# Sums over scores by halves of 512 columns, with gc tiles of two batches and gathers four slots ahead

## The chip, the cores and the metric

The kernel runs on one core of a Trainium2 chip, from one program in one launch. Its time is the device time of an execution in microseconds (us); lower is better. TensorE is called PE, VectorE DVE, ScalarE ACT, GpSimd POOL and SyncE SP, as in the profile. Everything is float32.

## What is computed

Sixteen graphs (batches) of 1024 nodes with 256 features each go through four layers; all share one 1024x1024 matrix adj, which has about 17 entries that aren't zero in a row. The reference, cut to what matters:

```python
# layer 0: a score for every edge, then two sums over neighbours
pre_u, pre_v = h @ W1[:d], h @ W1[d:]
S   = sigmoid(relu(pre_u[:, :, None] + pre_v[:, None] + b1) @ W2 + b2)
a_t = einsum('buv,bud->bvd', S * adj, h)
m_t = einsum('uv,bud->bvd', adj, h) * h
z   = beta1 * h + beta2 * (a_t @ Wa + ba) + beta3 * (m_t @ Wm + bm)
# layer 1
z = z + relu((adj @ z) @ W.T + b)
# layers 2 and 3: attention, each with its own weights
feats  = z @ W1.T;  f1 = feats @ W2 + b2
coefs  = softmax(leaky_relu(f1[:, :, None] + f1[:, None, :]) + adj)
z = coefs @ feats + bias2 + z
```

## The kernel before

The batches are worked in four groups of four (GB). A first part, `score_free`, makes for all 16 batches what layer 0 has besides the scores, and keeps it in DRAM (zb_d, and h·Wa as hw_d). Then each group runs `with_edges`, which adds the sums over scores onto z, and `group_layers`, which makes layers 1 to 3. The last group is worked in pairs of batches (`far_ahead`, `pair_layers`).

**Scores, on the side.** `score_steps` makes a group's scores one group ahead. A step takes one neighbour of each of 128 nodes in four batches: POOL gathers rows of v_d into a slot tile z of 4112 bytes a partition (`fetch`, L945), DVE takes a maximum, a minimum and a product with the tile u (L1065 to L1067), ACT sums the features of the four batches (L1033). Every 16 or 4 steps there are a tanh and a product with adj, and POOL scatters the scores into a dense matrix in DRAM, dense_d, whose innermost index is the batch (L950). 608 steps are made in all. The pool of slots has 6 tiles; LEAD = 5 says that the gather of step n + 5 is issued in step n, so it needs the slot that step n - 1 has left. The class `Side` emits so many of these steps beside each part of the main work as the table PACE says, and `paced` makes an instruction wait for a matmul some places back in PE's order, so that the side work keeps pace.

**Sums over scores, before.** For each group there are four quarters of 256 columns (v) and eight tiles of 128 rows (ut). One load (SP, `load_gd`, L1147, pool gd of four tiles) brings 128 x 256 x 4 scores; one copy turns them from column by batch into batch by column (gc, pool of two tiles): DVE makes it for ut 2, 4, 6 and 7 (L1496), ACT for the others (L1498). Then eight products, four batches by two halves of the output features, add into eight banks, each half full; that is all the banks there are. A float32 product shows as two matmul instructions in the profile. After the eighth ut DVE adds the eight banks onto z (L1521). Loads of the next z and of the turned adj into `ea`, and ACT's exponential of it, are strewn between.

**Other users of what changes.** `adj_stream` feeds layer 1 (seven products of quarters in place of eight, `seven`) with blocks of adj and of sums of its quarters: it puts pairs of blocks into gc tiles and single ones into a pool of three. Where it has more room (the first three groups) every second name goes to a wide tile. In the last group `by_lists` makes the neighbour sums of layer 1 for six tiles of nodes by gathering rows of y_d into the same slots (L945), adding them on DVE (L1716, L1718, L1714) and storing partial sums in part_d (L1722, on SP's queue).

Of the kernel before, what the change touches and what calls it, by code (L numbers as in the profile page):

```python
# [11 lines left out]
F32 = mybir.dt.float32  # L12
# [5 lines left out]
P = 128  # L18

GB = 4  # L20
# [12 lines left out]
HOLD = 52  # L33
FAR = 6
AHEAD = 3
LEAD = 5
LAG = 1
SOUGHT = 6
PLAIN = 3
# [41 lines left out]
def gnn_stack_kernel(  # L81
# [27 lines left out]
    nc = tc.nc  # L109
# [814 lines left out]
    with tc.If(listed > 0) as arm:  # L924
        with ExitStack() as stack:
# [4 lines left out]


            zs = stack.enter_context(tc.tile_pool(name="zs", bufs=2, reuse_waits="tile"))
            slot_pool = stack.enter_context(tc.tile_pool(name="slots", bufs=6, reuse_waits="tile"))
            wide_z = stack.enter_context(tc.tile_pool(name="wide_z", bufs=4, reuse_waits="tile"))
            wide_t = stack.enter_context(tc.tile_pool(name="wide_t", bufs=5, reuse_waits="tile"))
            psum_pool(stack, "banks", 8)
            gd_pool = stack.enter_context(tc.tile_pool(name="gd", bufs=4, reuse_waits="tile"))
            gc_pool = stack.enter_context(tc.tile_pool(name="gc", bufs=2, reuse_waits="tile"))
            searched = set()
            put = [Scatters(tc, f"scores {g}") for g in range(NGR)]  # L940
            finished = []
# [228 lines left out]
            with ExitStack() as first:  # L1170
# [60 lines left out]
                def score_free():  # L1231
# [58 lines left out]
                    for b in range(B):  # L1290
                        h, hT = kept.pop(0)
                        if b == 1:
                            nat = load_naturals(stage)
                            w1 = own1.tile([P, DH, 2 * R + D], F32, name="w1p")
                            nc.sync.dma_start(w1.rearrange("p c k -> p (c k)"), w_d)
                        mT = new_mT(pools)
                        rest = along_seven(b)
                        if b == B - 1:
                            first_hw.extend(load_hw(i) for i in range(GB - 1))
                        if b < PLAIN - 1:  # L1300
                            yield from first_turned(messages(pools, h, hT, mT=mT))
                        elif b == PLAIN - 1:
                            yield from last_plain(h, hT, mT)
                            sums = sums_of_adj()
                            rest = iter(())
                        else:
                            adding = itertools.chain(
                                adding, feature_sums(quarter, kept[0][0]) if b + 1 < B else iter(())
                            )
                            yield from mixed_in(messages(pools, h, hT, sums, quarter, mT), rest)  # L1310
                        if b == B - 1:
                            first_gd.extend(load_gd(0, 0, ut) for ut in range(4))
                        yield from rest
# [166 lines left out]
                yield 1.2  # L1480

            def exponential(jt):
                paced(nc.scalar.activation(ea[:, jt, :], ea[:, jt, :], AF.Exp), 16)

            def with_edges(g, hw, z):

                doing[0] = "edges"
                for v in range(N // QN):
                    cols = slice(v * QN, (v + 1) * QN)
                    acc = [[bank() for _ in range(DH)] for _ in range(GB)]  # L1490
                    for ut in range(NT):
                        gd = first_gd.pop(0) if first_gd else load_gd(g, v, ut, back=BACK)
                        gc = gc_pool.tile([P, GB, QN], F32, tag="gc", name="gc")
                        by_batch = gd.rearrange("p n i -> p i n")
                        if ut in (2, 4, 6, 7):
                            paced(nc.vector.tensor_copy(gc, by_batch), 16)  # L1496
                        else:
                            paced(nc.scalar.activation(gc, by_batch, AF.Copy), 16)  # L1498
                        for i in range(GB):
                            for eh in range(DH):  # L1500
                                product(
                                    acc[i][eh][:, :QN], hw[i][:, ut, eh * P : (eh + 1) * P], gc[:, i, :],
                                    start=ut == 0, stop=ut == NT - 1,
                                )
                        if z_loads and ut % 2 == 0:
                            load, *what = z_loads.pop(0)
                            paced(load(*what), 12)
                        if (to_load or to_exp) and ut % 2 and v:
                            if v > 1 and to_exp:
                                exponential(to_exp.pop(0))  # L1510
                            if to_load:
                                jt = to_load.pop(0)
                                paced(nc.sync.dma_start(ea[:, jt, :], adjT_d[jt]), 16)
                                to_exp.append(jt)
                        yield 3.4 if g or v else 1
                    if v == N // QN - 1:
                        while to_exp:
                            exponential(to_exp.pop(0))
                    for i in range(GB):
                        for eh in range(DH):  # L1520
                            nc.vector.scalar_tensor_tensor(  # L1521
                                z[i][:, eh, cols], acc[i][eh][:, :QN], zbias[:, eh : eh + 1], z[i][:, eh, cols],
                                ALU.add, ALU.add,
                            )

            def projected(z, keep=None, ticks=False, y=None):

# [45 lines left out]
            def adj_stream(room):  # L1573
# [31 lines left out]
                def block(name, k):  # L1605

                    if used:
                        q, was = used.pop()
                        if roomy is not None:
                            ask_for(q + 2, was) if q % 2 or was == 1 else was > 1 and single()  # L1610
                        elif was == 1:
                            ask_for(q + 2, was)
                        elif was > 1:
                            single()
                    used.append((names.index(name), k))
                    return ready[name, k]
# [13 lines left out]
                single(True)  # L1630
                single(True)
                ask(names[1], 0, HT if roomy is not None else 1, True)
                if roomy is not None:
                    ask(names[2], 0, first=True)
                single(True)
                return block

            def neighbours_by_seven(y, z, t, block):
# [42 lines left out]
            def by_lists(msg):  # L1681
# [16 lines left out]
                def fetch_row(t, k):  # L1698
# [4 lines left out]
                    else:  # L1703
                        gather(z, y_d, lists(t)[1][:, k : k + 1])

                for step in todo[:LEAD]:
                    fetch_row(*step)
                for n, (t, k) in enumerate(todo):
# [10 lines left out]
                            to, z, lists(t)[3][:, k : k + 1], to, ALU.mult, ALU.add  # L1719
                        ))  # L1720
                    if t >= NT and k == QUAD - 1:
                        nc.sync.dma_start(part_d[(t - NT) * P : (t - NT + 1) * P, :], to)  # L1722
                    yield 1.0

            def from_lists(z, msg):
# [145 lines left out]
            def soon(g):  # L1871

                if g in finished:
                    first_gd.extend(load_gd(g, 0, ut) for ut in range(4))

            def far_ahead(z, main):

# [161 lines left out]
```

## Time and profile before

| | us |
|---|---|
| median of three runs | 3041.68 |
| lowest and highest run | 3033.42, 3042.52 |
| the profiled execution | 3062.02 |
| its span, first to last instruction | 3059.9 |

The mean granted clock of TensorE in the profiled execution is 0.997. An engine's busy time is the union of its instructions; a group's line reads: line, engine, operation, written tile and read tiles, shapes, count, busy time in us and mean length of one in ns, then the idle time of the engine just before these instructions and what ended most of it. A matmul's mean length is longer than its share of the busy time, since matmuls overlap. In the view by windows a row has the stretch, its length, the busy time of PE, PEld, DVE, ACT and POOL with the number of instructions, the granted clock, the busy share of the DMA engines and GB/s. In a timeline a row has start, length, engine, line, operation, tiles and shape, and in brackets the idle time before and what ended it.

### The profile page before, as it was taken

How to read it: one execution, taken by the hardware profiler on the slowest of the kernel's cores; microseconds unless marked ns; L12 is line 12 of the kernel's file. 1: busy time of each engine (PE TensorE's matmuls, PEld its weight loads, DVE VectorE, ACT ScalarE, POOL GpSimd, SP SyncE). 2: the span in 40 equal slices, each digit the busy share in tenths (PEclk: the TensorE clock that was granted, in tenths of full speed). 3: DMA queues.
4: the chain of work that ended last, by engine and by line, in shares of the span. 5: the costliest groups of instructions: out<-in, count | busy, mean ns of one | idle time of the engine just before them, and what ended most of it. 6: DMA issues, size and time to landing. Idle time of an engine off the chain costs nothing. (4 is left out here: it accounts for less than half of the span.)

```text
span 3059.9 us, 41657 instructions
## 1 busy us (share of the span) xinstructions
PE 2994.9 (98%) x11774; PEld 2147.0 (70%) x11774; DVE 2080.4 (68%) x4093; ACT 1816.5 (59%) x6461; POOL 1717.0 (56%) x1481
## 2 busy tenths in 40 slices
PE   8999999999999999999999999999999999989999
PEld 5545555555557657888775788887578888848888
DVE  8877666666665678887667788766677752268844
ACT  3337665666666767887766678776667733214342
POOL 1137577677665667667676667666666520167500
PEclk9999999999999999999999999999999999999999
DMA  8899999889899976578998666898865445485500
GB/s 295 316 355 328 311 310 300 276 256 277 251 347 328 307 263 183 172 218 290 302 296 273 179 182 195 290 299 280 276 202 168 141 158 161 154 271 162 161 1 29
DMA packets 321145, 731.52 MB, mean 239 GB/s; under 512 B 50749, under 2 KB 145018, under 8 KB 315786
## 3 DMA queue, kind: packets, MB, share of 16 engines
q0 software_dynamic: 128064, 388.90, 42.1%
q1 hardware_dynamic: 154634, 271.98, 26.5%
q10 hardware_dynamic: 38208, 67.91, 5.9%
q8 instruction: 95, 1.56, 0.2%
q14 instruction: 144, 1.18, 0.1%
HBM read 592.10 MB, written 136.53 MB: 238 GB/s over the span
## 5 line engine op out<-in xcount | busy, mean ns | idle before, releaser
L1033 ACT ACTIVATE z<-z 128x257 f32<-128x257 f32 x2432 | 983.8, 410 | 529.7 <-DVE z L1067 290.8
L141 PE MATMUL bank<-feats,m 128*128 128x257 f32 x4096 | 912.3, 381 | 8.2 <-DVE m L1464 5.7
L141 PEld LDWEIGHTS bank<-feats,m 128*128 128x128 f32 x4096 | 769.5, 190 | 121.8 <-DVE m L1464 9.1
L945 POOL DMA_INDIRECT z<-v_d,slot_v x512 | 602.0, 1176 | 406.1 <-issue 149.0
L950 POOL DMA_INDIRECT dense_d<-gt,slot_at x512 | 595.2, 1162 | 220.3 <-issue 98.9
L1065 DVE TENSOR_TENSOR z<-z,u 128x580 f32<-128x580 f32 x608 | 461.2, 759 | 354.3 <-PE bank L141 259.2
L141 PE MATMUL bank<-gc,hw 128*128 128x256 f32 x2048 | 455.1, 384 | 20.8 <-ACT gc L1498 18.3
L1033 ACT ACTIVATION_READ_ACCUMULATOR z<-z 128x1 f32 x2432 | 467.1, 192 | 0.0
L141 PEld LDWEIGHTS bank<-gc,hw 128*128 128x128 f32 x2048 | 390.3, 192 | 85.0 <-ACT gc L1498 25.2
L1464 DVE SCALAR_TENSOR_TENSOR m<-rho,tau,adj_sb 128x512 f32<-128x512 f32 x512 | 375.0, 745 | 108.4 <-PE bank L141 98.5
L1066 DVE TENSOR_TENSOR z<-z,u 128x448 f32<-128x448 f32 x608 | 376.3, 619 | 0.0
L141 PE MATMUL bank<-w1p,hT 128*128 128x385 f32 x1024 | 340.1, 486 | 1.1 <-ACT hT L153 1.1
L141 PEld LDWEIGHTS bank<-w1p,hT 128*128 128x128 f32 x1024 | 193.1, 189 | 148.0 <-issue 22.0
L141 PE MATMUL bank<-g_wT,z 128*128 128x257 f32 x1024 | 231.0, 380 | 3.7 <-DVE z L1650 2.2
L141 PE MATMUL bank<-adj_sb,h 128*128 128x512 f32 x504 | 223.3, 592 | 1.1 <-DMA h<-in_x_dram 1.1
L141 PEld LDWEIGHTS bank<-g_wT,z 128*128 128x128 f32 x1024 | 191.9, 190 | 34.9 <-issue 4.4
L1498 ACT ACTIVATE gc<-gd 128x1024 f32<-128x1024 f32 x64 | 132.4, 2069 | 105.0 <-PE bank L141 90.3
L372 ACT ACTIVATE st<-bank 128x385 f32<-128x385 f32 x256 | 122.5, 483 | 105.7 <-PE bank L141 72.4
L141 PEld LDWEIGHTS bank<-adj_sb,h 128*128 128x128 f32 x504 | 95.5, 190 | 115.9 <-issue 106.5
L945 POOL DMA_INDIRECT z<-v_d,x_node x96 | 116.5, 1214 | 99.4 <-PE bank L141 32.4
L1067 DVE TENSOR_TENSOR z<-z,sign 128x128 f32<-128x128 f32 x608 | 172.2, 283 | 0.0
L1496 DVE COPY gc<-gd 128x1024 f32<-128x1024 f32 x64 | 71.5, 1118 | 139.4 <-PE bank L141 109.6
(248 smaller groups left out, 3311.4 us busy)
## 6 DMA issues: line engine op xcount, KB each, us to landing
gd<-dense_d SPq DMA_DIRECT2D x128, 512.0 KB
dense_d<-zero ACTq DMA_DIRECT2D x64, 512.0 KB
h<-in_x_dram SPq DMA_DIRECT2D x19, 1024.0 KB
u_d<-st SPq DMA_DIRECT2D x128, 128.5 KB
v_d<-st SPq DMA_DIRECT2D x128, 128.5 KB
u<-u_d POOLq DMA_DIRECT2D x32, 514.0 KB
hw_d<-st SPq DMA_DIRECT2D x128, 128.0 KB
zb_d<-zb ACTq DMA_DIRECT2D x16, 1024.0 KB
```

Source lines behind the costliest of these rows:

```text
L141: recent.append(nc.tensor.matmul(*args, **kw))
L372: nc.scalar.activation(st[:, cols], ps[:, :half], AF.Copy)
L945: return paced(nc.gpsimd.indirect_dma_start(out=dst, out_offset=None, in_=src[:], in_offset=bass.IndirectOffsetOnAxis(ap=at, axis=0), **how,))
L950: return paced(nc.gpsimd.indirect_dma_start(out=dst[:], out_offset=bass.IndirectOffsetOnAxis(ap=at, axis=0), in_=src, in_offset=None,))
L1033: nc.scalar.activation(zk[:, c, :], zk[:, c, :], AF.Copy, accum_out=s[:, k, c : c + 1])
L1065: paced(nc.vector.tensor_tensor(big, big, uk[:, :, :BIG], ALU.max))
L1066: paced(nc.vector.tensor_tensor(low, low, uk[:, :, BIG:], ALU.min))
L1067: nc.vector.tensor_tensor(mixed, mixed, sign[:, None, :].to_broadcast([P, GB, MIXED]), ALU.mult)
L1464: nc.vector.scalar_tensor_tensor(m, r[:, cols], ta[:, kt : kt + 1], ea[:, kt, cols], ALU.max, ALU.mult)
L1496: paced(nc.vector.tensor_copy(gc, by_batch), 16)
L1498: paced(nc.scalar.activation(gc, by_batch, AF.Copy), 16)
```

## The change

Five things are changed, the rest of the program is as it was.

- `with_edges` goes by halves of 512 columns. For each ut two loads bring the two quarters; a gc tile holds 512 columns of two batches, so that each load is copied in two parts, and each gc tile is filled by two copies. Of the four copies of a ut ACT makes one and DVE three. A product is 512 columns wide and fills a bank. The first two batches' banks are added onto z after their last product, the other two's after the copies of the next half's first ut.
- The gc pool has three tiles, the slot pool five in place of six, and LEAD is 4.
- Where an instruction was held to a matmul 24, 16 or 12 places back in this part, it is held to one 12, 8 or 6 back, since a product is twice as wide.
- `adj_stream` asks for three gc blocks at its start and runs three names ahead with them.
- `by_lists` stores part_d from ACT's queue, three steps after the sum is made.

```diff
-LEAD = 5
+LEAD = 4
...
-slot_pool = ... name="slots", bufs=6
+slot_pool = ... name="slots", bufs=5
-gc_pool = ... name="gc", bufs=2
+gc_pool = ... name="gc", bufs=3
...
-first_gd.extend(load_gd(0, 0, ut) for ut in range(4))
+first_gd.extend(load_gd(0, q, ut) for ut in range(2) for q in range(2))
...
 def with_edges(g, hw, z):
-    for v in range(N // QN):
-        acc = [[bank() for _ in range(DH)] for _ in range(GB)]
-        for ut in range(NT):
-            gd = first_gd.pop(0) if first_gd else load_gd(g, v, ut, back=BACK)
-            gc = gc_pool.tile([P, GB, QN], F32, tag="gc", name="gc")
-            by_batch = gd.rearrange("p n i -> p i n")
-            if ut in (2, 4, 6, 7):
-                paced(nc.vector.tensor_copy(gc, by_batch), 16)
-            else:
-                paced(nc.scalar.activation(gc, by_batch, AF.Copy), 16)
...
+    PB = GB // 2
+    acc, ended = {}, []
+
+    def copied(gds, pair):
+        gc = gc_pool.tile([P, GB, QN], F32, tag="gc", name="gc")
+        gc = gc.rearrange("p a b -> p (a b)").rearrange("p (i n) -> p i n", n=HN)
+        for q, gd in enumerate(gds):
+            to = gc[:, :, q * QN : (q + 1) * QN]
+            by_batch = gd.rearrange("p n i -> p i n")[:, pair * PB : (pair + 1) * PB, :]
+            if pair or q:
+                paced(nc.vector.tensor_copy(to, by_batch), 8)
+            else:
+                paced(nc.scalar.activation(to, by_batch, AF.Copy), 8)
+        return gc
+
+    def onto_z(pair, v):
+        cols = slice(v * HN, (v + 1) * HN)
+        for i in range(pair * PB, (pair + 1) * PB):
+            for eh in range(DH):
+                nc.vector.scalar_tensor_tensor(
+                    z[i][:, eh, cols], acc[i, eh], zbias[:, eh : eh + 1], z[i][:, eh, cols],
+                    ALU.add, ALU.add,
+                )
+
+    for v in range(NV):
+        for ut in range(NT):
+            gds = [first_gd.pop(0) if first_gd else load_gd(g, 2 * v + q, ut, back=12) for q in range(2)]
+            for pair in range(2):
+                gc = copied(gds, pair)
+                if ut == 0:
+                    while pair and ended:
+                        ended.pop()()
+                    for i in range(pair * PB, (pair + 1) * PB):
+                        for eh in range(DH):
+                            acc[i, eh] = bank()
+                for i in range(pair * PB, (pair + 1) * PB):
+                    for eh in range(DH):
+                        product(
+                            acc[i, eh], hw[i][:, ut, eh * P : (eh + 1) * P], gc[:, i - pair * PB, :],
+                            start=ut == 0, stop=ut == NT - 1,
+                        )
...
+                if ut == NT - 1 and not pair:
+                    onto_z(0, v)
+                yield 3.4 if g or v or ut >= NT // 2 else 1
+        ended.append(functools.partial(onto_z, 1, v))
...
+    ended.pop()()
...
 def adj_stream(room): # block(), start
-            if roomy is not None:
-                ask_for(q + 2, was) if q % 2 or was == 1 else was > 1 and single()
+            if roomy is not None and q % 2:
+                ask_for(q + 2, was)
             elif was == 1:
-                ask_for(q + 2, was)
+                ask_for(q + (3 if roomy is None else 6), 0)
...
+    ask(names[2], 0, first=True)
+    single(True)
     if roomy is not None:
-        ask(names[2], 0, first=True)
-    single(True)
+        ask(names[4], 0, first=True)
...
 def by_lists(msg):
-        nc.sync.dma_start(part_d[(t - NT) * P : (t - NT + 1) * P, :], to)
+        whole.append((n + 3, nc.scalar.dma_start, part_d[(t - NT) * P : (t - NT + 1) * P, :], to))
+    while whole and n >= whole[0][0]:
+        _, store, *what = whole.pop(0)
+        paced(store(*what))
```

In the built program the numbers of gathers, score steps and products by column are the same as before, and so, to within three steps, is the place of each stage among the score steps on DVE.

More of the change, by code (lines that the diff above doesn't have):

```diff
@@ L932, in gnn_stack_kernel @@
             zs = stack.enter_context(tc.tile_pool(name="zs", bufs=2, reuse_waits="tile"))
-            slot_pool = stack.enter_context(tc.tile_pool(name="slots", bufs=6, reuse_waits="tile"))
+            slot_pool = stack.enter_context(tc.tile_pool(name="slots", bufs=5, reuse_waits="tile"))
             wide_z = stack.enter_context(tc.tile_pool(name="wide_z", bufs=4, reuse_waits="tile"))
@@ L937, in gnn_stack_kernel @@
             gd_pool = stack.enter_context(tc.tile_pool(name="gd", bufs=4, reuse_waits="tile"))
-            gc_pool = stack.enter_context(tc.tile_pool(name="gc", bufs=2, reuse_waits="tile"))
+            gc_pool = stack.enter_context(tc.tile_pool(name="gc", bufs=3, reuse_waits="tile"))
             searched = set()
@@ L1482, in exponential @@
             def exponential(jt):
-                paced(nc.scalar.activation(ea[:, jt, :], ea[:, jt, :], AF.Exp), 16)
+                paced(nc.scalar.activation(ea[:, jt, :], ea[:, jt, :], AF.Exp), 8)
             def with_edges(g, hw, z):
                 doing[0] = "edges"
-                for v in range(N // QN):
-                    cols = slice(v * QN, (v + 1) * QN)
-                    acc = [[bank() for _ in range(DH)] for _ in range(GB)]
-                    for ut in range(NT):
-                        gd = first_gd.pop(0) if first_gd else load_gd(g, v, ut, back=BACK)
-                        gc = gc_pool.tile([P, GB, QN], F32, tag="gc", name="gc")
-                        by_batch = gd.rearrange("p n i -> p i n")
-                        if ut in (2, 4, 6, 7):
-                            paced(nc.vector.tensor_copy(gc, by_batch), 16)
-                        else:
[L1498 to L1519, printed above, removed]
@@ L1520, in with_edges @@
+                def onto_z(pair, v):
+                    cols = slice(v * HN, (v + 1) * HN)
+                    for i in range(pair * PB, (pair + 1) * PB):
                         for eh in range(DH):
                             nc.vector.scalar_tensor_tensor(
-                                z[i][:, eh, cols], acc[i][eh][:, :QN], zbias[:, eh : eh + 1], z[i][:, eh, cols],
+                                z[i][:, eh, cols], acc[i, eh], zbias[:, eh : eh + 1], z[i][:, eh, cols],
                                 ALU.add, ALU.add,
@@ L1524, in with_edges @@
                             )
+                for v in range(NV):
[15 more added lines that the diff above has]
+                                    )
+                            if z_loads and not pair:
+                                load, *what = z_loads.pop(0)
+                                paced(load(*what), 6)
+                            if (to_load or to_exp) and pair and (v or ut >= NT // 2):
+                                if v and to_exp:
+                                    exponential(to_exp.pop(0))
+                                if to_load:
+                                    jt = to_load.pop(0)
+                                    paced(nc.sync.dma_start(ea[:, jt, :], adjT_d[jt]), 8)
+                                    to_exp.append(jt)
+                            if ut == NT - 1 and not pair:
+                                onto_z(0, v)
+                            yield 3.4 if g or v or ut >= NT // 2 else 1
+                    ended.append(functools.partial(onto_z, 1, v))
@@ L1526, in projected @@
+                while to_exp:
+                    exponential(to_exp.pop(0))
+                ended.pop()()
             def projected(z, keep=None, ticks=False, y=None):
@@ L1704, in fetch_row @@
                         gather(z, y_d, lists(t)[1][:, k : k + 1])
+                whole = []
                 for step in todo[:LEAD]:
@@ L1873, in soon @@
                 if g in finished:
-                    first_gd.extend(load_gd(g, 0, ut) for ut in range(4))
+                    first_gd.extend(load_gd(g, q, ut) for ut in range(2) for q in range(2))
             def far_ahead(z, main):
```

## The prediction, on record before the changed kernel ran

> **What bounds the kernel now.** I read the busy times first, then the stages that the change touches, then what ends the idle time of the engine that is full. All durations are of the profiled execution: 3062.02 us, its span 3059.9 us. The median of the three timed runs is 3041.68 us, 20.3 us lower; I work out a difference inside the profile and take it from the median.
>
> ```profile
> PE 2994.9 (98%) x11774; PEld 2147.0 (70%) x11774; DVE 2080.4 (68%) x4093; ACT 1816.5 (59%) x6461; POOL 1717.0 (56%) x1481
> ...
> L141 PE MATMUL bank<-gc,hw 128*128 128x256 f32 x2048 | 455.1, 384 | 20.8 <-ACT gc L1498 18.3
> ...
> L141 PE MATMUL bank<-adj_sb,h 128*128 128x512 f32 x504 | 223.3, 592 | 1.1 <-DMA h<-in_x_dram 1.1
> ...
> L1498 ACT ACTIVATE gc<-gd 128x1024 f32<-128x1024 f32 x64 | 132.4, 2069 | 105.0 <-PE bank L141 90.3
> ...
> L1496 DVE COPY gc<-gd 128x1024 f32<-128x1024 f32 x64 | 71.5, 1118 | 139.4 <-PE bank L141 109.6
> ```
>
> PE is the bound: 2994.9 of 3059.9 us, 65 us idle. The sums over scores (out bank, in gc and hw) hold 20.8 us of this idle time, and 18.3 of it ended when an ACT copy into gc ended. So the reader is to look at PE's waits in the four edge stages and nowhere else first. The stretches from the first to the last of these matmuls, in the view by windows (columns: length; busy time of PE, PEld, DVE, ACT, POOL; granted clock; DMA share; GB/s):
>
> ```profile
> 904.00:1029.00 125.00, 116.43 (x514) 98.81 (x513) 70.71 (x130) 85.09 (x248) 62.44 (x51) 0.97 0.95 333
> 1449.00:1569.00 120.00, 113.14 (x519) 96.71 (x518) 74.48 (x141) 80.67 (x253) 81.84 (x66) 1.00 0.93 304
> 1992.00:2114.00 122.00, 116.61 (x520) 99.45 (x519) 76.76 (x147) 86.05 (x278) 82.42 (x64) 0.97 0.90 300
> 2534.00:2645.00 111.00, 111.00 (x518) 97.77 (x517) 32.77 (x52) 29.25 (x16) 0.52 (x1) 1.00 0.48 154
> ```
>
> The same 512 matmuls take 111 us where no score steps run beside them and 125, 120 and 122 us where they do: 14 + 9 + 11 = **34 us** lost. About 7 us of it is the clock (0.97 of 125 and of 122 us), which falls after the larger waits. No other stage has as much to give.
>
> **Sums by 512 columns.** One matmul of 256 columns is 455.1/2048 = 0.2222 us, one of 512 columns 223.3/504 = 0.4431 us. 1024 wide ones in place of 2048: 1024 x (0.4444 - 0.4431) = **-1 us**. PE's work by columns is the same; only waits can be saved.
>
> **Three gc tiles of two batches.** A gc tile is now 16 matmuls, 3.56 us of PE; a new one is 8 matmuls of 0.4431, 3.54 us. With two tiles a copy may begin only when PE has left the tile before the last, so it has 3.56 us, of which ACT's takes 2.07; whatever stands before it on ACT (four score sums, 4 x 0.41 us; a 1028-column u row, 1.05 us) eats the rest. With three tiles it has 7.1 us. The copies become 256 of 512 elements: 64 on ACT at about 1.05 us (half of 2069, and the 1.05 us of the u row), 67 us for 132; 192 on DVE between half of 1118 and the 745 of the 512-column m row, taken near the half, 0.59: 113 us for 71.5. The additions onto z go from 128 x 0.479 to 64 x 0.742 (the row of L499, as wide): 7 us less. Per stage DVE gains 9 us on 71 to 77 of some 120, ACT loses 16 of 81 to 86. Neither is full, so I cost this beside PE at nothing; if DVE's cover went, it would be these 9 us in three stages, 27.
>
> ScalarE's activation with immediate operands should take 186 ns and 0.833 ns an element, by the Trainium skill (ScalarE: Activation LUTs, What ACT_TABLE_LOAD costs): 1039 ns for 1024 elements, an estimate, where the row has 2069; this read, of every fourth word, is outside that rule. By the page a half copy would save ACT 27 us in all instead of 65; the sum below doesn't change, since ACT is only relieved.
>
> What is left is the other cause of these waits. The longest, 4.4 us near 944 us, is not a lack of buffers:
>
> ```profile
> 946.49 2.01 ACT L1498 ACTIVATE gc<-gd 128x1024 f32<-128x1024 f32 x1 [4.71 <-DMA gd<-dense_d]
> ```
>
> ```profile
> 949.21 1.08 DVE L1496 COPY gc<-gd 128x1024 f32<-128x1024 f32 x1 [8.38 <-DMA gd<-dense_d]
> ```
>
> Both copies stood for the load of gd. The change doesn't make loads earlier: they hang on the matmul 12 wide products back, as far as 24 narrow ones, and gd keeps four tiles; a tile pair must now be whole before its first copy. So of the 34 us between nothing (all of it loads) and all 34 (all of it buffers) can go. The page gives no landing of gd; I took the packets of 4096 bytes of queue q1 in order, 128 to a load. In the first stage the copies behind PE's waits for ACT (7.6 us in 5 waits) began mostly within 1.3 us of the landing: loads, with the DMA engines 0.95 busy. In the second and third gd had landed 1.9 to 15.7 us before the copy that PE waited for (10.8 us in 8 waits), and ACT was at score sums: buffers. I leave the first stage its 14 us and take the 9 + 11 = 20 of the others.
>
> The early addition of two batches frees four banks 3.5 us before the other four; banks end only 0.4 us of PE's idle time today: no gain. It waits on PE at DVE, and in the built program a copy and a score step stand behind it: some 3.3 us of DVE's work under 3.5 us of PE's. Little is to spare; I put 0.5 us on each of the six ends of a half beside scores (bounds 0 and the 1.7 us of a score step): 3 us. So **-17 us** in the edge stages.
>
> **Four gathers ahead, five slots.** This pays for the third gc tile. Each step gathers one z row (POOL, 1.18 us), DVE's max waits for it, and today DVE waits little: 8.4 us in 6 times for z<-v_d. The page gives no landing for these; taking the packets of 4112 bytes of queue q0 in order, 128 to a gather, a row lands 4.6 us (median; 7.8 in the 95th of 100) after POOL's instruction, and DVE takes it up 10.2 us later (the 5th of 100: 2.8). One slot fewer takes one step, 3.8 us on average, from that: 35 of 608 would come late, by 43 us together, 18 of them before 500 us. Bounds 0 and 43 us. DVE already stands 259.2 us waiting for PE before the same max, and PE has three m tiles (3 x 8 matmuls of 0.2227 = 5.3 us) of cover, so I take the low end, **+4 us**.
>
> **The last group.** SP stands for three stores of part_d, and the loads behind them come late to PE (first fence SP, second PE):
>
> ```profile
> 2685.39 13.72 SPq L1722 DMA_DIRECT2D part_d<-msg  x3
> 2699.21 1.39 SPq L1597 DMA_DIRECT2D adjT_in<-sumT_d  x3
> ```
>
> ```profile
> 2707.72 7.13 PE L141 MATMUL bank<-adjT_in,t 128*128 128x512 f32 x16 [3.68 <-DMA adjT_in<-sumT_d]
> ...
> 2716.28 1.98 PE L141 MATMUL bank<-adjT_in,t 128*128 128x512 f32 x4 [1.43 <-DMA adjT_in<-sumT_d]
> ```
>
> The stores go to ACT's queue, three steps later, when what they wait for is mostly done; behind them there stand the relu of four banks and y copies, for which PE waits. And a third block is asked for ahead. 5.1 us at most, less about 1 on ACT: **-4 us** (bounds 0 and -5). DMAs issued from different engines run on the same DMA engines, so spreading them saves only issue time, says the Trainium skill (DMA: Bandwidth & Descriptors, Issuing engines are not separate DMA queues). By that rule this term is nothing; the row says that SP's time was waiting, which a queue of its own does save. The row gathers of the lists land mostly 0.2 to 2.4 us before their use between 2705 and 2740 us (by their packets, as above); with five slots for six their cycle grows by up to 0.25 us in 40 steps, 10 us on DVE: **+2 us** at PE (bounds 0 and 10). In the groups before, no adjT_in wait stands today, so more blocks ahead give nothing; the last asked stands on SP behind the end of the edge stage, under the 14 us of projections.
>
> **Sum:** -1 - 17 + 4 - 4 + 2 = -16 us: 3046 for the profiled execution, **3026 us** for the median. Runs of this kernel tell 0.3%, 9.1 us, from no change.
>
> **Rivals.** (1) The waits are loads, not buffers: a faster PE asks a DMA that is 0.95 busy for more, and -17 shrinks to -5. For it: the fence of 946 us, and that pairs must be whole. Against: the 10.8 us of waits with gd long landed. Sum -4: 3038 us, no difference that can be told; the change then doesn't do what it is built for. (2) Slots starve: late rows stop DVE, in order, and with it m and the copies, so that half of the 43 us (21) and all 10 us of the lists reach PE, while edge stages give 8 and stores 2: -1 - 8 - 2 + 21 + 10 = +20, 3062 us. It decides from where DVE's delay passes the 5.3 us that three m tiles cover. (3) All 34 us are buffers, nothing is lost: -1 - 34 - 5 = -40, 3002 us.
>
> **Chances.** Forecast (-9 to -27 us, 3015 to 3033) 0.46; (1) 0.25; (2) 0.17; (3) 0.12. Faster 0.46 + 0.12 = 0.58, the same 0.25, slower 0.17. The range from 3003 to 3052 us leaves out most of (2) and the end of (3), under 0.2.
>
> **What would show it.** Right: the three slow stages at 115 to 119 us, PE's idle time before gc,hw under 10 us, no 13.72 us stand on SP, DVE's waits for z<-v_d from 8 to some 30 us. Wrong: these stages still at 120 or more, with gd named as what ended the copies' idle time (1); or waits for DVE m and z at PE between 200 and 900 us or in the sums, which are few today (5.7 us for m) (2).

## The result, and the profile after

Before, the median was 3041.68 us; after the change it is **3069.68 us** (five runs of each on one chip), a ratio of 1.0100 with a 95% interval of 1.0077 to 1.0124. On another chip the same pair gave 1.0088 (1.0063 to 1.0112). The kernel is slower by about 1%, some 28 us; the prediction was 3026 us, and 3069.68 lies outside its range. The profiled execution took 3072.16 us, its span 3070.3 us.

From the page of the kernel after: the busy times, and the groups of the sums and of DVE's copies into gc.

```profile
PE 2995.5 (98%) x10750; PEld 1956.2 (64%) x10750; DVE 2115.0 (69%) x4157; ACT 1764.4 (57%) x6461; POOL 1708.6 (56%) x1481
...
L141 PE MATMUL bank<-gc,hw 128*128 128x512 f32 x1024 | 453.9, 603 | 30.9 <-DVE gc L1498 28.4
...
L1498 DVE COPY gc<-gd 128x512 f32<-128x512 f32 x192 | 115.4, 634 | 191.3 <-DMA gd<-dense_d 171.1
```

PE's idle time before these matmuls was 20.8 us and is now 30.9, and DVE's copies stand in its place where ACT's stood. ACT is relieved by 52 us (its copies alone by 60.5, where 65 were costed) and DVE has 35 us more, as costed; neither engine is full. The four edge stages after, by windows (columns as in the table of before):

```profile
910.00:1037.00 127.00, 116.11 (x258) 50.00 (x257) 76.17 (x146) 72.98 (x245) 64.02 (x52) 0.96 0.96 343
1457.00:1578.50 121.50, 111.82 (x258) 47.76 (x257) 77.23 (x154) 67.29 (x248) 85.09 (x67) 1.00 0.90 302
2001.50:2127.50 126.00, 115.69 (x259) 48.82 (x257) 81.69 (x163) 73.90 (x278) 84.42 (x65) 0.97 0.90 304
2544.50:2654.50 110.00, 110.00 (x260) 48.87 (x259) 38.87 (x65) 17.28 (x16) 0.89 (x1) 1.00 0.49 155
```

The stage without score steps is 1 us shorter, as wide matmuls should make it. The three others were to fall to 115 to 119 us; they are 2, 1.5 and 4 us longer by these windows (2.4, 2.2 and 4.9 us from the first matmul's start to the last one's end). The waits (engine, written tile and line, what it waited for: us in all, times, longest), first before the change and then after it:

```profile
DVE gc L1496 <- DMA gd<-dense_d: 25.0, 8, 8.4
...
DVE z L1065 <- DMA z<-v_d,slot_v: 8.4, 6, 2.5
...
ACT gc L1498 <- DMA gd<-dense_d: 8.0, 5, 4.7
```

```profile
DVE gc L1498 <- DMA gd<-dense_d: 171.1, 47, 8.8
...
ACT gc L1500 <- DMA gd<-dense_d: 105.9, 27, 8.6
DVE z L1065 <- DMA z<-v_d,slot_v: 54.1, 24, 7.0
...
DVE z L1065 <- DMA z<-v_d,x_node: 20.5, 10, 6.0
```

Copies stand for a load 277 us, where before it was 33. The maximum stands for gathered rows 54.1 us, where it was 8.4. The first, with stages over 120 us, is the mark that the prediction had named for rival (1). The second passes the 30 us that it allowed for being right; of its mark for (2), waits of PE for DVE's m and z, little is to be seen (1.3 us for m, which was 5.7; one wait of 4.8 us for mT). What either costs is not yet said by a list of waits.

### The profile page after: what moved, and what is told of

The parts are those of the page before. It is cut to its first block, busy times and chain, and to the rows that moved or that the text cites. A ratio compares the mean times of both kernels' runs of the same rounds, so it can differ in the third digit from the quotient of the medians.

```text
span 3070.3 us, 39732 instructions
## 1 busy us (share of the span) xinstructions
PE 2995.5 (98%) x10750; PEld 1956.2 (64%) x10750; DVE 2115.0 (69%) x4157; ACT 1764.4 (57%) x6461; POOL 1708.6 (56%) x1481
## 5 line engine op out<-in xcount | busy, mean ns | idle before, releaser
L1033 ACT ACTIVATE z<-z 128x257 f32<-128x257 f32 x2432 | 984.7, 410 | 572.1 <-DVE z L1067 362.3
L950 POOL DMA_INDIRECT dense_d<-gt,slot_at x512 | 578.4, 1130 | 206.9 <-PE bank L141 110.9
L141 PE MATMUL bank<-gc,hw 128*128 128x512 f32 x1024 | 453.9, 603 | 30.9 <-DVE gc L1498 28.4
L1033 ACT ACTIVATION_READ_ACCUMULATOR z<-z 128x1 f32 x2432 | 466.2, 192 | 0.0
L141 PEld LDWEIGHTS bank<-gc,hw 128*128 128x128 f32 x1024 | 194.9, 193 | 287.6 <-issue 249.7
L1498 DVE COPY gc<-gd 128x512 f32<-128x512 f32 x192 | 115.4, 634 | 191.3 <-DMA gd<-dense_d 171.1
L945 POOL DMA_INDIRECT z<-v_d,x_node x96 | 125.7, 1310 | 123.1 <-ACT z L1033 59.2
L141 PE MATMUL bank<-adjT_in,t 128*128 128x512 f32 x352 | 154.5, 592 | 0.0
```

The source lines that it names most:

```text
L141: recent.append(nc.tensor.matmul(*args, **kw))
L945: return paced(nc.gpsimd.indirect_dma_start(out=dst, out_offset=None, in_=src[:], in_offset=bass.IndirectOffsetOnAxis(ap=at, axis=0), **how,))
L950: return paced(nc.gpsimd.indirect_dma_start(out=dst[:], out_offset=bass.IndirectOffsetOnAxis(ap=at, axis=0), in_=src, in_offset=None,))
L1033: nc.scalar.activation(zk[:, c, :], zk[:, c, :], AF.Copy, accum_out=s[:, k, c : c + 1])
L1498: paced(nc.vector.tensor_copy(to, by_batch), 8)
```

## The experiments

**Two theories.** L, the loads: two loads must be in before a pair of gc tiles can be filled, and they are asked for no earlier than before. S, the slots: with five slots and gathers four ahead the rows come late. Every kernel ran with a kernel before beside it on the same chip, since chips differ (before had medians of 3042 to 3067 us); so ratios are compared. Where a span is split up I use **PE's loss**: from the start of each matmul to the start of the next, less the median for its kind, summed. It holds PE's waits and the stretches at half clock. Span less loss is 2976 to 2980 us in every kernel shown here, so that all differences between them are loss, but for these 4 us.

| kernel | ratio to before (95%) | loss in the edge stages, us | elsewhere, us |
|---|---|---|---|
| before, first profile | | 32.9 | 47.1 |
| before_again | 1.0005 (0.9991 to 1.0018) | 29.4 | 55.2 |
| after, first profile | 1.0100 (1.0077 to 1.0124) | 44.9 | 49.1 |
| after_again | 1.0088 (1.0063 to 1.0112) | 39.5 | 67.3 |
| before_lead4 | 1.0045 (1.0027 to 1.0063) | 30.4 | 69.5 |
| before_three_gc | 1.0079 (1.0066 to 1.0092) | 35.5 | 49.8 |
| before_back48 | 0.9973 (0.9964 to 0.9982) | 22.7 | 33.3 |
| before_new_lists | 0.9999 (0.9983 to 1.0015) | 28.9 | 45.8 |
| wide_alone | 1.0008 (0.9992 to 1.0024) | 39.1 | 50.5 |
| wide_lists | 1.0002 (0.9993 to 1.0012) | 42.8 | 28.4 |
| after_gc2 | 1.0093 (1.0078 to 1.0107) | 39.5 | 44.2 |
| after_old_blocks | 1.0104 (1.0076 to 1.0132) | 41.6 | 70.4 |
| after_back20 | 1.0007 (0.9992 to 1.0023) | 19.8 | 74.9 |
| wide_lists_back20 | 0.9943 (0.9923 to 0.9963) | 16.3 | 46.1 |
| wide_lists_back24 | 0.9933 (0.9920 to 0.9945) | 16.4 | 31.4 |
| wide24_again | 0.9931 (0.9918 to 0.9944) | 14.2 | 28.2 |
| wide24_old_lists | 0.9948 (0.9934 to 0.9961) | 18.2 | 29.0 |
| wide24_lead4 | 0.9940 (0.9926 to 0.9953) | 18.8 | 30.9 |
| wide24_slots5 | 1.0006 (0.9997 to 1.0015) | 27.7 | 41.6 |

A loss is that of one profiled execution, and "elsewhere" differs by some 15 us from chip to chip; a ratio rests on all runs.

**Before once more, and its slots alone.** before_again has no edit; before_lead4, in the kernel before:

```diff
-LEAD = 5
+LEAD = 4
-slot_pool = ... bufs=6
+slot_pool = ... bufs=5
```

> The kernel before once more, for a second profile. The first profiled execution took 3062.02 us, 20 us over the median, so a stall seen in it may not be typical. Both theories: the time as before within 0.3%. Theory L (loads in pairs: the changed kernel is slower because both loads of gd must land before the first copy) expects the three edge stages beside scores to be as short or shorter here than the 124.5, 119.5 and 121.2 us of the first profile, some 115 to 120, so that the changed kernel's 126.9, 121.7 and 126.1 us are a loss of 20 us or so. Theory S (slots: the changed kernel is slower because gathers come late) expects the stages here as in the first profile, and what is gained in this execution to lie outside them.

> The kernel before with LEAD 4 and five slots, nothing else. Theory S: most of the loss is in this one edit, 15 to 28 us slower than before, with DVE's wait for z<-v_d at 50 us or more (8.4 before, 54.1 after). Theory L: 0 to 8 us slower, though DVE's wait for z grows as much.

Five slots with gathers four ahead, in the kernel before, cost 0.45%, 14 us, between the two forecasts. They do it outside the edge stages (30.4 us there, as without; 69.5 elsewhere). S holds for half of the loss.

**The wide sums alone, and the change with earlier loads.** wide_alone has the new `with_edges` but two gc tiles, six slots, gathers five ahead, the old block stream and the old stores. Against the kernel after:

```diff
-LEAD = 4
+LEAD = 5
-slot_pool = ... bufs=5
+slot_pool = ... bufs=6
-gc_pool = ... bufs=3
+gc_pool = ... bufs=2
...
-                ask_for(q + (3 if roomy is None else 6), 0)
+                ask_for(q + 2, was)
...
-            whole.append((n + 3, nc.scalar.dma_start, part_d[...], to))
+            nc.sync.dma_start(part_d[...], to)
```

after_back20 is the changed kernel with one edit:

```diff
-            gds = [... load_gd(g, 2 * v + q, ut, back=12) for q in range(2)]
+            gds = [... load_gd(g, 2 * v + q, ut, back=20) for q in range(2)]
```

> The new sums by 512 columns with gc tiles of two batches and the early addition, but two gc tiles, six slots, LEAD 5 and the old block stream and list stores. Theory L: 20 us or more slower than before, with DVE and ACT standing for gd some 250 us in all (33 before, 277 after), since pairs of loads are the cause and here there is even one tile fewer. Theory S: within 10 us of before, since the slots are back.

> The changed kernel with the loads of gd held to the matmul 20 places back in place of 12, so that they may go out up to 7 us earlier as far as the four gd tiles allow. Theory L: DVE's and ACT's wait for gd falls from 277 us to under 120, PE's wait for the copies from 29.6 us to under 10, and 15 to 25 us of the loss come back. Theory S: PE's waits in the edge stages may shrink, but the time stays within 8 us of the changed kernel's, since late gathers still stop DVE.

In the edge stages the wide sums alone give back little: these are 126.4, 125.1 and 117.6 us, and PE loses 39.1 us in them, 10 more than in before_again. The time, though, is that of before (1.0008), as S had forecast and not L: without the change of slots the kernel isn't slower, since in these two profiles 7 of the 10 us are made up outside the stages and by the wide matmuls. With loads eight products earlier the changed kernel has lost all its disadvantage too (1.0007; the stages are 115.2, 117.7 and 116.9 us), with the late rows still there (43.4 us of waiting for v_d). L holds as well: either edit alone takes the loss away.

**The parts together.** after_again has no edit. wide_lists_back20 has the wide sums with `back=20`, six slots, LEAD 5, two gc tiles and old blocks as wide_alone, and the stores on ACT as the kernel after. The other two put one part each into a whole kernel, before_new_lists into the kernel before and after_old_blocks into the kernel after:

```diff
-            nc.sync.dma_start(part_d[...], to)
+            whole.append((n + 3, nc.scalar.dma_start, part_d[...], to))
```

```diff
-                ask_for(q + (3 if roomy is None else 6), 0)
+                ask_for(q + 2, was)
```

> The changed kernel once more, beside the kernels of this chip. If its loss belongs to the program it is 1.008 to 1.012 of the kernel before here too (+25 to +37 us of 3067), with the edge stages at 125 to 128, 120 to 124, 124 to 128 and 110 us. Theory L (both loads of a pair must be in, and they are asked for too late) then gives it about 27 us above the same kernel with loads asked for 20 products back (1.0007), that is everything by which that one was better; theory S (late gathers) gives 14 us of the loss to the slots, which the earlier loads didn't touch. If it is under 1.004 here, the first result was one of the chip or of the moment, and only the 14 us of the slots are left to explain.

> The wide sums with two gc tiles, six slots and gathers five ahead, the blocks of layer 1 as before, the partial sums stored from ACT's queue, loads asked for 20 products back in place of 12. If L and S together are the whole loss, this has neither: edge stages at 115 to 119 us (-10 to -15 us against before), gathers as before (z waiting for v_d 8 to 12 us), and -4 us by the stores: 3046 to 3057 us, ratio 0.993 to 0.997. If wide products with pairs of loads lose by something else as well (copies of two engines into one tile, four additions at the end of a half, two gc tiles being too few for pairs), it is 1.000 or more and the edge stages stay over 120 us.

> The kernel before with only the partial sums stored from ACT's queue, three steps later. By the step of the prediction: SP's stand of 13.7 us at the third store is gone, so are PE's waits for adjT_in<-sumT_d (3.7 and 1.4 us), and the time falls by 3 to 5 us, ratio 0.9984 to 0.9990. By the rival that the wait only moves (to ACT, behind whose stores relu and y copies stand, or to the next load), it is 0.9995 to 1.0005.

> The changed kernel with the blocks of layer 1 asked for as before the change (two names ahead, the third gc tile unused there). If asking three names ahead is worth nothing, as the prediction had it, the ratio is that of the changed kernel within 0.001. If the early blocks crowd the queue or the DMA engines where gathers and loads of z are due, this is 5 to 10 us faster than the changed kernel; if the third block helps the last group, 3 to 5 us slower.

The loss is the program's own on a second chip. Without L and S the wide form is 0.57% **faster** than before. The blocks three names ahead make no difference that these runs tell (1.0104 beside 1.0088). The stores alone gain nothing in the kernel before (0.9999), where 3 to 5 us were forecast. SP's 13.7 us stand for part_d is gone in before_new_lists, but another has taken its place, and PE waits as before (first fence SP, second PE):

```profile
2671.12 26.35 SPq L1597 DMA_DIRECT2D adjT_in<-sumT_d  x4
```

```profile
2700.87 4.54 PE L141 MATMUL bank<-adjT_in,t 128*128 128x512 f32 x6 [3.95 <-DMA adjT_in<-sumT_d]
```

SP now reaches the loads of sums early and stands 26.35 us over four of them, longer than before; the load that PE needs comes no earlier. Of the rule that I weighed there, the Trainium skill (DMA: Bandwidth & Descriptors, Issuing engines are not separate DMA queues), the outcome was right, though not by its reason: SP's waiting was real, it was only not the last wait.

**Loads, gc tiles and slots one at a time.** wide_lists and wide_lists_back24 are wide_lists_back20 with `back=12` and `back=24`. before_three_gc is before_lead4, and after_gc2 after_old_blocks, with one edit each:

```diff
-gc_pool = ... bufs=2
+gc_pool = ... bufs=3
```

```diff
-gc_pool = ... bufs=3
+gc_pool = ... bufs=2
```

> As wide_lists_back20, but with its loads asked for 12 products back as in the changed kernel; two gc tiles, six slots, gathers five ahead. If the place of the loads is what makes the edge stages, PE loses 37 to 45 us in them (wide_lists_back20: 16.3, the kernel before: 29.4) and the ratio is 0.999 to 1.003, against 0.994 there. If the early loads did little and the stores on ACT's queue did the rest, it is 0.993 to 0.996.

> As wide_lists_back20, with loads asked for 24 products back, as early as the list of products allows. Theory L with nothing left behind it: gd is there in any case and the four tiles of gd are the limit; edge stages and time as at 20 back, ratio 0.992 to 0.996. The rival, that earlier loads push gathers and loads of z aside (the DMA engines are nearly full in the first edge stage), gives late gathers (z waiting for v_d over 20 us) and 0.996 to 1.000.

> The narrow sums of before with three gc tiles for two, and, since they don't fit otherwise, five slots and gathers four ahead. By the prediction's step on buffers, PE's waits in the second and third edge stage are for gc tiles: the third tile takes some 17 to 20 us of them away, which with the slots' 14 us gives 0.998 to 1.000 and PE's loss in the edge stages falls from 30 to 10 or 15 us. By the rival, that those waits are loads and copies standing behind other work on ACT, not tiles, it is as with five slots alone: 1.003 to 1.006, and 26 to 32 us lost in the edge stages.

> The changed kernel with two gc tiles for three, and layer 1's blocks asked for as before the change; five slots, loads 12 back. With loads as late as that a third tile can't be filled earlier than its load comes: if so, the ratio is that of the changed kernel, 1.008 to 1.012, and 38 to 45 us are lost in the edge stages. If the third tile was worth what the prediction gave it, this is 10 to 20 us slower than the changed kernel, 1.012 to 1.016.

These four ran on one chip, so three steps can be read off. wide_lists to wide_lists_back24 changes the place of the loads alone: 1.0002 to 0.9933, 23 us, with the loss in the edge stages from 42.8 to 16.4 us. wide_lists to after_gc2 takes one slot and one step of lead: 1.0002 to 1.0093, 25 us. And after_gc2 to the changed kernel, which ran on other chips, adds the third gc tile and the blocks: 1.0093 beside 1.0088 and 1.0100, nothing.

The best version by windows, on the chip of its last run (wide24_again):

```profile
902.00:1018.50 116.50, 111.72 (x259) 48.13 (x258) 76.33 (x145) 72.10 (x244) 59.07 (x52) 1.00 1.00 363
1435.50:1551.50 116.00, 110.52 (x260) 48.63 (x259) 78.95 (x155) 68.09 (x250) 79.39 (x66) 1.00 0.94 319
1968.50:2080.50 112.00, 110.78 (x261) 48.85 (x260) 82.55 (x164) 74.26 (x277) 84.15 (x65) 1.00 0.96 336
```

The DMA engines stood at 0.96, 0.90 and 0.90 after the change and are at 1.00, 0.94 and 0.96 here: the first stage moved 343 GB/s and now 363. So these loads were not limited by what the DMA engines can carry, which was rival (1)'s reason; they were asked for too late.

Three gc tiles in the narrow form (before_three_gc) were the test of the step that the whole prediction rested on, and it fails: the stages are 126.8, 116.4 and 123.3 us, the loss 35.5 us where 10 to 15 were to be left. In before_lead4, which has one gc tile less, they are 121.7, 117.3 and 123.8 us: the second and third stage, in which the prediction saw a lack of buffers, gain 0.9 and 0.5 us. The time, 1.0079, is even above what the rival had forecast (1.003 to 1.006), with 5 us more spent in the first stage; why is open. The waits of its copies show why one is easily misled:

```profile
DVE gc L1496 <- DMA gd<-dense_d: 136.4, 42, 7.9
...
ACT gc L1498 <- DMA gd<-dense_d: 93.6, 27, 8.6
...
ACT gc L1498 <- PE bank L141: 22.7, 8, 5.5
DVE gc L1496 <- PE bank L141: 21.2, 9, 5.1
```

With two tiles these copies waited for PE to leave a gc tile (109.6 and 90.3 us in the first profile of before) and rarely for a load. With three they wait for the load (136.4 and 93.6) and rarely for PE. The name of the releaser changed and PE's loss did not fall: a copy that was let go by the later of two events is let go by the other, hardly earlier. So the 277 us of the kernel after are no measure of its loss; after_gc2 has 114 us of them and the same time.

**Early loads in the narrow form, slots and lead apart, stores in the best version.** before_back48, against the kernel before:

```diff
-        del recent[:-BACK]
+        del recent[:-48]
...
-            gd = first_gd.pop(0) if first_gd else load_gd(g, v, ut, back=BACK)
+            gd = first_gd.pop(0) if first_gd else load_gd(g, v, ut, back=48)
```

The others are wide_lists_back24 with one thing changed: wide24_lead4 with `LEAD = 4`, wide24_slots5 with that and `bufs=5` for the slots, wide24_old_lists with the stores of part_d on SP's queue again, wide24_again with nothing.

> The kernel before, narrow sums, with its loads of scores held to 48 narrow products back in place of 24 (24 wide ones in time), nothing else. If the lateness of the loads is the whole matter of the edge stages, with wide or with narrow products, they come down to 112 to 118 us here too, PE loses 15 to 20 us in them in place of 29, and the ratio is 0.994 to 0.997. If the narrow form was held by its gc tiles and by copies behind other work on ACT, as the prediction had it for the second and third stage, the loads change little: 0.998 to 1.001, and only the wide form gains by early loads.

> The best version so far (wide sums, two gc tiles, loads 24 back: 0.9933) with gathers four steps ahead in place of five, but still six slots. If what costs 0.6 to 0.9 per cent with five slots is the time from the gather's issue to its use, this has all of it: 0.999 to 1.003, z waiting for v_d 40 to 65 us. If it is the slot that POOL waits for, it has nothing of it: 0.992 to 0.995, z waiting for v_d 10 to 20 us.

> The best version so far (0.9933) with the partial sums stored from SP's queue again, as before the change. If moving the stores is worth as little here as it was in the kernel before (0.9999), the ratio is 0.992 to 0.9955 and PE's waits for adjT_in<-sumT_d may be back by up to 5 us. If it carries part of the gain, it is 0.996 to 0.998.

> Wide sums, two gc tiles, loads 24 products back, gathers four ahead (0.9940 with six slots), now with five slots: one tile less and nothing else. If it is the tile that costs, POOL's stands for a slot with the sum on ACT before it pass 5 us again where DVE was held up just before (near 325 us: 7 us with five slots, at most 2.1 us with six), PE's waits for mT near 337 us (6 to 7 us with half the clock after) and for st near 1935 us come back, and the ratio is 0.999 to 1.002. If five slots only cost together with late loads or a third gc tile, it stays at 0.993 to 0.996.

> The best version once more, on the chip of its rival with five slots: wide sums, two gc tiles, six slots, gathers five ahead, loads 24 back, partial sums stored from ACT's queue. If its gain is its own, 0.992 to 0.9945; if it was one of the chip, above 0.997.

The kernel before with its loads hung on a product twice as far back is 0.27% faster. Its stages by windows:

```profile
906.50:1029.00 122.50, 114.00 (x513) 97.61 (x512) 69.66 (x129) 85.22 (x252) 63.43 (x51) 0.99 0.96 344
1446.00:1561.00 115.00, 112.41 (x518) 97.06 (x517) 74.68 (x141) 80.66 (x252) 79.61 (x65) 1.00 0.95 318
1977.50:2095.50 118.00, 112.53 (x517) 96.63 (x516) 76.11 (x146) 85.33 (x275) 82.10 (x63) 1.00 0.91 304
```

The time and the loss of 22.7 us lie between the two forecasts. The second and third stage, which the prediction gave to gc tiles, fall to 115 and 118 us by loads, below all five other profiles of the narrow sums (116.4 to 119.9 and 120.2 to 123.8 us); the first, which it gave to loads, stays within theirs (121.7 to 126.8). So the attribution fails in all three, though a stage that differs by 3 us from one profile to the next can't size the gain well. In the first stage the narrow form does have another limit, which the wide form hasn't (116.5): its cause, ACT's 2.07 us copies behind score sums being my guess, was not tried.

In the best version the stores moved to ACT differ by 0.15%, some 5 us (0.9948 beside 0.9933 and 0.9931). That is the size of the prediction's -4, but the intervals overlap: not shown.

The slots gave the surprise. With six slots and gathers four ahead the rows come as late as with five, and less than 0.1% is lost: 0.9940. The expectation had tied late rows and lost time together; the waits came out by its first case and the time by its second. One tile less is 1.0006, 20 us. The maximum's waits of wide24_lead4, and then of wide24_slots5:

```profile
DVE z L1065 <- DMA z<-v_d,slot_v: 55.4, 28, 7.5
```

```profile
DVE z L1065 <- DMA z<-v_d,slot_v: 58.1, 31, 4.7
```

So 55 us of DVE's waiting for rows are as good as free. The waits for the other kind of rows do differ, wide24_lead4 first:

```profile
DVE z L1065 <- DMA z<-v_d,x_node: 2.9, 2, 2.2
```

```profile
DVE z L1065 <- DMA z<-v_d,x_node: 15.2, 9, 2.9
```

What differs most is POOL. Its waits for a slot (the sum L1033 on ACT is the slot's last reader), for wide24_lead4, wide24_slots5 and wide_lists_back24:

```profile
POOL z L945 <- ACT z L1033: 119.0, 112, 12.0
```

```profile
POOL z L945 <- ACT z L1033: 218.2, 166, 9.8
```

```profile
POOL z L945 <- ACT z L1033: 219.8, 163, 12.0
```

The best version stands for slots as long as the one with five, but its rows are asked for five steps ahead. With six slots and four steps POOL stands half as long. In these three only both together, a POOL that stands and rows with little to spare (the maximum waits 13.2 us for them in wide_lists_back24), cost time. One place shows how, in wide24_slots5: POOL, then DVE, then PE.

```profile
318.05 0.94 POOL L945 DMA_INDIRECT z<-v_d,slot_v  x1 [0.47 <-ACT z L1033]
324.44 4.48 POOL L945 DMA_INDIRECT z<-v_d,slot_v  x1 [5.45 <-ACT z L1033]
```

```profile
320.39 0.18 DVE L1713 TENSOR_SCALAR to_u<-to_u 128x32 uint32<-128x32 uint32 x1 [4.96 <-DMA extra_d<-xrows,to_u]
...
333.65 0.76 DVE L1065 TENSOR_TENSOR z<-z,u 128x580 f32<-128x580 f32 x1 [4.43 <-DMA z<-v_d,slot_v]
```

```profile
340.62 1.10 PE L141 MATMUL bank<-sums,t 128*128 128x512 f32 x1 [3.77 <-DVE mT L422]
```

DVE stands 4.96 us for a scatter, so the sum that frees the slot is late, POOL stands 5.45 us, its gather takes 4.48 us more and the row lands after 333; DVE stands again, 4.43 and then 3.33 us, the product mT behind it is late, and PE loses 3.77 us and then runs 3.5 us at a granted clock of 0.54. The scatter itself had left POOL at 314.27 us, here behind stands of 2.93 and 1.06 us for slots, and at 311.04 in wide24_lead4, where DVE stands 2.06 us for it, POOL nowhere over 2.1 us for a slot between 200 and 600 us, and PE not at all. The same chain is in the profile of the kernel after, where PE waits 4.81 us for mT at 339.66. That it stands for all 20 us is not shown: the profiles of the two kernels differ by 8.9 us of loss in the edge stages and 10.7 elsewhere, at many small places.

The wide sums with two gc tiles and the stores on ACT's queue now have all four cases of loads and slots:

| ratio to before | loads 12 products back | loads 24 back |
|---|---|---|
| six slots, gathers five ahead | 1.0002 (wide_lists) | 0.9933, 0.9931 |
| five slots, gathers four ahead | 1.0093 (after_gc2) | 1.0006 (wide24_slots5) |

Late loads cost 0.7 to 0.9% with either number of slots, and the slots 0.7 to 0.9% with either place of the loads: the two costs add, some 21 to 28 us each. So the wide sums are worth a gain of 0.7%, and the changed kernel lays both costs on it. The third gc tile is worth nothing beside early loads either: after_back20 has it, with five slots and loads 20 back, and takes 1.0007 beside the 1.0006 of wide24_slots5. Three gc tiles with six slots were not run.

## Why the prediction was wrong, point by point

**The edge stages, -17 us.** This step failed. "Of the 34 us between nothing (all of it loads) and all 34 (all of it buffers) can go": it left out that the range goes below nothing. The prediction wrote down both facts that decide it, that the change doesn't make loads earlier and that a pair must be whole before its first copy, and then used them only for the first stage. Measured: three stages got 2.4, 2.2 and 4.9 us longer, the fourth 0.7 shorter, PE's loss in them went from 32.9 to 44.9 us (29.4 to 39.5 on the later chips), **+10 to +12**. In the whole time the wide sums with late loads came out at **0 to +2 us** (wide_lists 1.0002, wide_alone 1.0008), where -18 with the width were forecast; it is the early loads, which the change didn't have, that bring the stages to 112 to 117 us, where 115 to 119 were forecast. The reason that led astray was to call PE's waits of the second and third stage waits for buffers, since gd "had landed 1.9 to 15.7 us before the copy" and ACT was at score sums. before_three_gc gives them the buffer and gains nothing in time; before_back48 gives them the loads and gains 5 and 2 us against the second profile of before (119.9 and 120.2 us), 5 and 3 against the first. A row that has landed before one copy says nothing of what set the time of the copies before it.

**Slots, +4 us.** The bounds 0 to 43 held, the choice didn't: 14 us in the kernel before, 20 to 25 in the wide form. "PE has three m tiles (...) of cover, so I take the low end" looks at late rows alone, and they are free (wide24_lead4); it left out that a late sum holds POOL, and POOL the next gathers and scatters, as at the place shown. The 43 us were the sum of the rows' lateness, so the bound was of the wrong quantity; that it holds the measured cost is luck. The whole miss is 44 us (-16 forecast, +28 measured). From the kernel before to wide_lists 22 us were to be gained (edge stages, width and stores) and nothing was; from there to after_gc2 slots and lists were to cost 6 and cost 25.

**The last group, -4 us.** The 13.72 us stand went, as forecast, and PE's loss behind the last edge stage stayed: 17.7 us before, 17.5 after. In before_new_lists it was not the last wait: SP stood 26.35 us over the next loads instead. In the kernel after, the loss from the first to the last product with adjT_in and t did go, from 6.2 us to nothing (11.3 to 1.3 in the second profiles), and as much was lost around it; why is open. Whether -4 is there in the wide form the runs don't tell.

**Wide matmuls, -1 us**, came at 0.7 us in the stage without score steps, some 3 us in four (an estimate). What was costed at nothing (copies on DVE and ACT, blocks ahead) cannot be seen to cost anything, though DVE's copies are now what PE waits for. In that step the additions' "7 us less" are right by busy time (54.6 to 47.5 us; measured 45.7), while the mean lengths printed there give 14. **Lists, +2 us**, cannot be told apart from the slots.

**The rivals.** (1) and (2) both happened, (1) in a stronger form and by another reason: it kept 5 us of gain in the stages where 10 were lost, and it blamed full DMA engines, which carried the same loads earlier. Of (2) the slots' cost is there, but late rows alone don't make it (wide24_lead4). They had been priced as alternatives, each with the rest of the forecast left standing, though nothing in them excludes the other. Taken together with the prediction's own prices, -1 for the width, -5 and -2, and (2)'s +21 and +10, they give +23 us, 3065, near the 3069.68 measured and outside the range; as in time its terms for the edge stages and the width are off by 6 to 8 us and those for rows and lists by some 6 to 11 the other way, that it comes so near is in part luck. (3) is refuted by before_three_gc.

## What to carry to other kernels

A wait with two conditions is named by the later one. Before a buffer is added for it, look at when the other condition came: if that is a load issued from the same pace, the buffer only changes the name. Here the wide sums with loads asked for 24 products back and six slots with gathers five ahead (at the price of the third gc tile, for which no run shows a gain) turn a loss of 1% into a gain of 0.7% (0.9931, 0.9918 to 0.9944; 3020.51 us where before had 3043.50); with either of the two alone the time is that of before.

When a pool in a ring through several engines is made smaller, price the engine that stands for the tile and all that is queued behind it, not only the one that uses the data. And add rivals up where they don't exclude each other.

## What the runs showed of the hardware

A short wait of PE can cost as much again by the clock. In before_again PE waited 1.86 us at 952 us and then had half the clock for 3.4 us, which is another 1.7 us; columns as in the windows above:

```profile
950.50:954.00 3.50, 1.64 (x8) 1.11 (x7) 0.00 (x0) 2.81 (x5) 1.02 (x2) 1.00 1.06 267
954.00:957.40 3.40, 3.40 (x10) 2.66 (x9) 2.48 (x4) 0.35 (x2) 1.44 (x1) 0.50 1.02 400
```

The Trainium skill (TensorE: Matmul & The Clock Gate, What's actually happening) puts the fall of the clock after an idle window of about 3.4 us. The length of the half-clock stretch agrees: 3.41 us or twice that within the profiles of before_again and the kernel after; that it takes 3.4 us of idleness does not: here 1.86 us were enough, while other waits of 2.5 us (1492 us in wide24_again) brought none.

Chips differ by PE's waits and not by how fast it works, as far as two profiles show: the kernel before had medians of 3041.68 and 3066.68 us on two chips, while span less PE's loss was 2980 and 2978 us.
